# Attention block: probabilities turned by products with a diagonal of reciprocals instead of the identity

## The chip, the cores and the metric

One core of a Trainium2 chip runs the whole kernel. The metric is the device time of one execution in microseconds (us); the profile shows one execution, taken by the hardware profiler.

## The reference, cut to what matters

For x of shape (4, 1024, 1024) in f32, the block is `x + s * g`, where s is attention over the normalized x and g the SiLU of a feed-forward branch of the same input. The change concerns the attention alone:

```python
xn = _layernorm(x, axis=-1)
q = (xn @ Wq.T) ...        # 16 heads of 64, in 4 groups of 4 that share a key head
k, v = (xn @ Wk.T) ..., (xn @ Wv.T) ...
att = einsum('bkgqd,bkjd->bkgqj', q, k) * scale
mask = causal & (j >= i - 511) | (j < 4) ...   # window of 512 keys and 4 sink keys
att = softmax(where(mask, att, -inf), axis=-1)
y = einsum('bkgqj,bkjd->bkgqd', att, v)
s = y.reshape(b, t, c) @ Wo.T
```

The softmax divides each row of probabilities by its sum. That division can be made on the exponentials, or later on y, since every key of a query has the same divisor.

## The kernel before, in words

The work runs in stages: normalizing x and making keys and values (to about 270 us), queries and the gate (to 949 us), attention, with the small feed-forward branch for the last token streamed between its products (949 to 1741 us), and the output projection with the gated sum (to the end).

In the attention stage the queries are tiles of 128. Each batch has eight; they are taken in pairs (`PAIRED`), a *far* tile (tiles 7 to 4, whose window of 512 keys lies apart from the 4 sink keys) and a *near* tile (tiles 0 to 3, with 1 to 4 blocks of 128 keys). A *step* (class `Step`) treats, for such a pair of tiles, two query heads `r` of two key heads `g`; there are 16 pairs of tiles and 4 steps of each, 64 steps. The loop over `p` (L1317 on) writes out the order of all engines but SP by hand (`tc.manual_schedule`): while the values of step p are multiplied, the scores, maxima and exponentials of step p + 1 are made (`far_next`, `near_next`).

For a step the engines do this:

- `scored` (L277, products at L299): PE multiplies the queries (64 rows of a head as weights, 128 columns) by the keys, into the PSUM tile `S`. Where the near tile of the next step has at most two blocks of keys, its scores *ride* in the free columns of the far tile's `S` (`riding`, `ride`); this is so in 31 steps of the loop, and they have another order of work.
- `merged` and `maxed` (L314, L335): DVE merges the own block of a far tile and takes masked row maxima; it writes the negated scores to `pr` in SBUF.
- `powered` (L346): ACT makes the exponentials in place, and the row sums into `sums`.
- `sinks_kept` (L351): POOL copies the 4 sink columns of the exponentials into a zeroed tile `held`.
- `turned` (L369): PE turns blocks of 128 queries by 128 keys so that the keys lie on the partitions. `in_halves` does it in two halves of 64 queries, each a `transpose` of 64 rows of `pr` with the identity, into the PSUM tile `t`; ACT then copies `t` to `pT` in SBUF (L383). One call turns one or two blocks of keys, 8 transposes for each block.
- `values`, `values_apart` (L411, L427): PE multiplies `pT`, the sinks and a correction of the first block (`lead`) by the values, into the PSUM tile `yp`.
- `stored` (L434): DVE writes `yp` to SBUF, multiplied by the turned reciprocals `scales`; `sent` sends it to DRAM.

The reciprocals of the row sums come from `inverted` (L471): DVE inverts the 8 columns of sums of a step (far and near together), and POOL spreads each over 64 columns (tile `r`). `turned_extras` (L482) turns `held` and the four spread pieces, 10 transposes in a step, and ACT copies them to `extras` (tile `e`, 128x640, L497): its first part are the turned sinks, the others the `scales` that `stored` multiplies by. The turned pieces go to a PSUM tile of their own (`et`) in riding steps, and to the free columns of the next far tile's `S` in the others.

The feed-forward branch is a generator; `streamed(least, most)` puts some of its blocks of products on PE (L1099) at fixed places of a step, and `small_products` its small transposing products (L1161).

Of the kernel before, what the change touches and what calls it, by code (L numbers as in the profile page):

```python
# [8 lines left out]
F32 = mybir.dt.float32  # L9
AF = mybir.ActivationFunctionType  # L10
ALU = mybir.AluOpType
# [4 lines left out]
P = 128  # L16
N_HEAD = 16
N_KV = 4
HS = 64
# [25 lines left out]
def recurrent_block_kernel(  # L45
# [170 lines left out]
    def make_masks():  # L216
        first = pools["first"]

        m = masks["near"] = first.tile([P, SCOLS], F32, name="near_mask")
        nc.gpsimd.memset(m, 0.0)  # L220
        nc.gpsimd.affine_select(
            out=m[:, OWN:], in_=m[:, OWN:], compare_op=ALU.is_ge, fill=NEG,
            base=0, pattern=[[-1, P]], channel_multiplier=1,
        )
        masks["far"] = m[:, :OWN]
        masks["own"] = triangle(first, "own_keys", ALU.is_ge, 1)
        masks["lead"] = triangle(first, "lead_keys", ALU.is_gt, 1)

        m = masks["full"] = first.tile([P, SINK], F32, name="full_mask")
        nc.gpsimd.memset(m, 0.0)  # L230
        nc.gpsimd.affine_select(
            out=m, in_=m, compare_op=ALU.is_ge, fill=NEG,
            base=0, pattern=[[-1, SINK]], channel_multiplier=1,
        )
# [17 lines left out]
    class Step:  # L252
# [89 lines left out]
        def powered(self, *heads):  # L342

            for r, g in heads:
# [3 lines left out]
                    accum_out=self.sums[:, r, g : g + 1],  # L348
                )

        def sinks_kept(self):  # L351

            self.held = held_sinks[(PAIR * self.m + self.rp) % 2]
            nc.gpsimd.tensor_copy(
                self.held.rearrange("p (g r k) -> p g r k", g=2, r=PAIR)[
                    :, :, :, QUAD - SINK :
                ],
                self.pr[:, :, :, WINDOW:],
            )

        def in_halves(self, ps, slot, src, n):

            for h in range(2):
                rows = slice(h * HS, (h + 1) * HS)
                nc.tensor.transpose(  # L365
                    ps[:n, h, slot * HS : (slot + 1) * HS], src[rows], ident[rows, rows]
                )

        def turned(self, *keys):  # L369

            ps = pools["ps_t"].tile([P, 2, WIDE], F32, tag="T", name=f"t{self.name}_{keys[0]}")
            slots = 2 * PAIR * len(keys)
            for n, k in enumerate(keys):
                for g in range(2):
                    for r in range(PAIR):
                        self.in_halves(
                            ps, (n * 2 + g) * PAIR + r,
                            self.pr[:, g, r, k * P : (k + 1) * P], P,
                        )
            pT = pools["px"].tile(  # L380
                [P, 2, 2, PAIR * P], F32, tag="pT", name=f"pT{self.name}_{keys[0]}", bufs=2
            )
            nc.scalar.copy(  # L383
                pT.rearrange("p k g c -> p (k g c)")[:, : slots * P].rearrange(
                    "p (s h q) -> p h s q", h=2, q=HS
                ),
                ps[:, :, : slots * HS].rearrange("p h (s q) -> p h s q", q=HS),
            )
            for n, k in enumerate(keys):
                self.pT[k] = pT[:, n]  # L390
# [32 lines left out]
        def values_apart(self):  # L423

            for r in range(PAIR):
                for _, rows, cols in self.quads():
                    nc.tensor.matmul(  # L427
                        self.y[rows, r * P : (r + 1) * P],
                        sink_values[self.b][:, r, cols], self.extras[:, 0, :],
                        start=False, stop=False, skip_group_check=True,  # L430
                    )
            self.added(self.lead, leads[self.i], False, True)

        def stored(self):  # L434
            if self.rp == 0:
                state[self.i] = pools["px"].tile(
                    [P, GROUP, P], F32, tag="y", name=f"y{self.i}_{self.m}", bufs=3
                )
            at = self.rp * PAIR
            nc.vector.tensor_tensor(  # L440
                state[self.i][:, at : at + PAIR, :],
                self.y.rearrange("p (r q) -> p r q", r=PAIR), self.scales, ALU.mult,
            )

        def sent(self):
# [22 lines left out]
        y = pools["ps_y"].tile([P, 2, PAIR * P], F32, tag="y", name=f"yp{far.name}")  # L468
        far.y, near.y = y[:, 0, :], y[:, 1, :]

    def inverted(steps, sums):  # L471

        name = steps[0].name
        inverse = pools["px"].tile([P, 2 * PAIR * 2], F32, tag="inverse", name=f"i{name}", bufs=2)
        nc.vector.reciprocal(inverse, sums.rearrange("p s r g -> p (s r g)"))  # L475
        spread = pools["px"].tile([P, 2 * PAIR * 2, HS], F32, tag="spread", name=f"r{name}", bufs=1)
        nc.gpsimd.tensor_copy(  # L477
            spread, inverse.unsqueeze(2).to_broadcast([P, 2 * PAIR * 2, HS])
        )
        return spread.rearrange("p (s g) c -> p s (g c)", g=2)  # L480

    def turned_extras(steps, spread, behind):  # L482

        far, near = steps
        parts = [far.held, *(spread[:, s, :] for s in range(2 * PAIR))]
        if behind is None:
            ps = pools["ps_t"].tile([P, 2, WIDE], F32, tag="T", name=f"et{far.name}")
        else:
            ps = behind.S[:, 0, :, SCOLS:]
        for slot, src in enumerate(parts):  # L490
            far.in_halves(ps, slot, src, P)
        extras = pools["px"].tile([P, len(parts), P], F32, tag="extras", name=f"e{far.name}", bufs=1)
        far.extras = extras
        far.scales, near.scales = extras[:, 1 : 1 + PAIR, :], extras[:, 1 + PAIR :, :]

        def kept():
            nc.scalar.copy(  # L497
                extras.rearrange("p s (h q) -> p h s q", h=2),
                ps[:, :, : len(parts) * HS].rearrange("p h (s q) -> p h s q", q=HS),
            )  # L500

        return kept

    PLACE = {0: 0, 1: 1, 2: 2, 3: 4, 4: 5, 5: 6, 6: 3}
# [10 lines left out]
    with ExitStack() as a:  # L520
# [445 lines left out]
        with tc.manual_schedule():  # L966
# [4 lines left out]
            for at, (kind, pair) in enumerate(passes):  # L971
# [35 lines left out]
                for k, i in enumerate(OUTER):  # L1007
# [16 lines left out]
                    if end and k == 3:  # L1024
                        early.close()
                        second_banks.close()
                        pools["first"] = attention_only.enter_context(
                            tc.tile_pool(name="first", bufs=1, side="right")
                        )
                        pools["ps_s"] = attention_only.enter_context(  # L1030
                            tc.tile_pool(name="ps_s", bufs=1, space=PSUM, side="right")
                        )
                        attention_inputs()
                        (far, near), sums_now = steps_of(*order[0])
                        def scores(step, rs):
                            step.scored(rs)
                            step.merged(rs)
                            step.maxed(rs)
                            step.powered(*((r, g) for r in rs for g in range(2)))

                        first_scores = iter((
                            lambda: scores(far, (0,)), lambda: scores(far, (1,)),
                            far.sinks_kept, lambda: scores(near, both),
                        ))
            for part in first_scores:
                part()
# [11 lines left out]
    with ExitStack() as a:  # L1058
# [255 lines left out]
        with tc.manual_schedule(  # L1314
            engines={engines.PE, engines.DVE, engines.Activation, engines.Pool}
        ):
            for p in range(len(order)):  # L1317
# [56 lines left out]
                small_products(far_next.S if more else None)  # L1374
                if last_near is not None:
                    last_near.sent()
                if rode:
                    spread = inverted((far, near), sums_now)
                if more:
                    far_next.merged((0,))  # L1380
                    far_next.maxed((0,))
# [2 lines left out]
                if more:  # L1384
                    far_next.powered((0, 0))
                if not rode:
                    spread = inverted((far, near), sums_now)
                far.led()
                streamed(1, 1)
                summed_in_one_bank(far, near)  # L1390
# [2 lines left out]
                if ride:  # L1393
# [4 lines left out]
                    near_next.powered((0, 0), (0, 1))  # L1398
                    far_next.scored((1,))
                    near_next.riding(1, far_next)  # L1400
                    turned_extras((far, near), spread, None)()
                    far_next.merged((1,))
                    far_next.maxed((1,))
                    near_next.maxed((1,))
                    far_next.powered((1, 0), (1, 1))
                    near_next.powered((1, 0), (1, 1))
                    far_next.sinks_kept()
                    if n_near <= 2:
                        streamed(0, 2)
# [10 lines left out]
                else:  # L1420
                    far.turned(2, 3)
                    late_passes()
                    if more:
                        far_next.powered((0, 1))
                        far_next.scored((1,))
                    kept = turned_extras((far, near), spread, far_next if more else None)
                    if more:
                        far_next.merged((1,))
                    kept()
                    if more:  # L1430
                        far_next.maxed((1,))
                        far_next.powered((1, 0), (1, 1))
                        far_next.sinks_kept()
                    streamed(0, 1)
                    for k in (2, 3):
                        far.values(k)
                    far.values_apart()
                    far.stored()
                    far.sent()
                    near.turned(*range(min(2, n_near)))  # L1440
                    if more:
# [292 lines left out]
```

## Time and profile before

| | |
|---|---|
| time, median of 3 runs | 2139.3 us (2134.91 to 2139.39) |
| the profiled execution: its own time | 2139.05 us |
| the profiled execution: its span | 2137.3 us |
| TensorE (PE) busy | 2076.3 us |
| weight loads (PEld) busy | 1418.0 us |
| VectorE (DVE) busy | 1495.8 us |
| ScalarE (ACT) busy | 916.5 us |
| GpSimd (POOL) busy | 448.4 us |
| HBM | 202 GB/s over the span |

A row of a group in the profile reads: line, engine, operation, out<-in by the program's names, the tile of the array for products (rows * columns), the shape, xcount | busy us, mean ns of one | idle time of the engine just before, and what ended it. Busy time counts overlapping instructions once; the mean is the length of a single one, of which a product's pipeline is a part. `PEld` are the loads of weights into the array, which overlap the products (`PE`). In `t<-ident,pr` the second name, `pr`, is the operand that is loaded as weights, and `ident` the one that is streamed. A timeline row gives start, length, engine, line, operation and count of instructions that follow each other.

### The profile page before, as it was taken

What the parts mean: (1) busy time and instruction counts of PE and PEld (TensorE: products, weight loads), DVE (VectorE), ACT (ScalarE), POOL (GpSimd) and SP (SyncE); (2) the same over time, 40 slices, a digit from 0 to 9 for tenths busy, and PEclk for the clock granted to TensorE, in tenths of its full rate; (3) what the DMA queues carried; (4) which work ended last, traced back from release to release, by engine and by line L of the source; (5) the groups of instructions that cost most, each with busy time, mean ns of one, the idle gap of its engine ahead of it and who ended that gap; (6) DMA issues with size and microseconds to landing.
All of it is one profiled execution on the core that took longest, in us unless ns stands there. A gap on an engine that the chain in (4) does not pass through costs nothing.

```text
span 2137.3 us, 43582 instructions
## 1 busy us (share of the span) xinstructions
PE 2076.3 (97%) x17586; PEld 1418.0 (66%) x17586; DVE 1495.8 (70%) x3092; ACT 916.5 (43%) x1840; POOL 448.4 (21%) x641
## 2 busy tenths in 40 slices
PE   7999999999999999999999999999999989999999
PEld 6888888888888888875555655555565544444443
DVE  5867588888877888876556555666665547777766
ACT  4343212111110000037777777777777744333332
POOL 3232315435241021141111111111111101111111
PEclk9999999999999999999999999999999999999999
DMA  8696322433554234258778988768578536666653
GB/s 297 248 370 218 104 99 99 163 114 124 224 188 138 99 110 166 79 190 290 261 237 240 319 250 243 256 198 301 185 251 284 182 146 180 167 169 191 172 157 98
DMA packets 215201, 417.20 MB, mean 195 GB/s; under 512 B 13796, under 2 KB 97844, under 8 KB 209880
## 3 DMA queue, kind: packets, MB, share of 16 engines
q1 hardware_dynamic: 171432, 266.12, 38.8%
q0 software_dynamic: 28288, 91.41, 13.8%
q10 hardware_dynamic: 15280, 56.89, 7.1%
q8 instruction: 138, 2.26, 0.4%
q14 instruction: 63, 0.52, 0.1%
HBM read 309.22 MB, written 121.93 MB: 202 GB/s over the span
## 4 chain that ended last, share of the span: by engine, by line
PE 83%; DVE 6%; issue 4%; ACT 4%; POOL 2%; DMA 1%; SPq 0%; ACTq 0%; POOLq 0%; DVEq 0%
PE u L1572 17%; PE u_q L899 16%; PE u_g L899 13%; PE S L299 10%; PE yp L411 8%; PE d_ps L1099 6%; PE t L365 5%; PE u L679 4%; PE yp L427 1%; DVE pr L335 1%; ACT pr L346 1%; ACT pT L383 1%; DVE t_g L915 1%; DVE f L852 1%; PE xtp L595 1%
## 5 line engine op out<-in xcount | busy, mean ns | idle before, releaser
L346 ACT ACTIVATE pr<-pr,nm 128x516 f32<-128x516 f32 (+4 forms) x512 | 325.5, 638 | 86.8 <-DVE nm L335 85.7
L335 DVE CUSTOM_DVE_ANT_0 pr<-S,near_mask 128x516 f32<-128x516 f32 (+4 forms) x512 | 275.7, 590 | 98.2 <-PE S L299 56.0
L383 ACT COPY pT<-t 128x1024 f32<-128x1024 f32 (+1 forms) x224 | 212.0, 946 | 116.5 <-PE t L365 114.5
L299 PE MATMUL S<-kT,qT 64*128 64x512 f32 (+4 forms) x1536 | 246.4, 446 | 4.0 <-DVE i L475 2.4
L411 PE MATMUL yp<-pT,v 128*32 128x256 f32 x3328 | 215.2, 382 | 5.1 <-ACT pT L383 4.5
L899 PE MATMUL u_q<-f,wq_again 128*128 128x256 f32 x896 | 203.2, 379 | 0.0
L899 PE MATMUL u_g<-wg,f 128*128 128x256 f32 x864 | 195.7, 380 | 4.5 <-DVE t_g L915 4.5
L365 PEld LDWEIGHTS t<-ident,pr 64*128 64x128 f32 x3328 | 126.1, 140 | 90.6 <-issue 68.6
L411 PEld LDWEIGHTS yp<-pT,v 128*32 128x32 f32 x3328 | 104.1, 110 | 123.4 <-issue 51.7
L899 PEld LDWEIGHTS u_q<-f,wq_again 128*128 128x128 f32 x896 | 170.0, 190 | 23.3
L899 PEld LDWEIGHTS u_g<-wg,f 128*128 128x128 f32 x864 | 163.8, 190 | 28.2 <-DVE t_g L915 6.2
L299 PEld LDWEIGHTS S<-kT,qT 64*128 64x128 f32 x1536 | 127.6, 190 | 79.2 <-issue 69.8
L1572 PE MATMUL u<-wo_sb,y 128*128 128x512 f32 x384 | 170.1, 592 | 0.5 <-DVE y L440 0.5
L365 PE MATMUL t<-ident,pr 64*128 64x64 f32 x3328 | 153.1, 230 | 4.0 <-ACT pr L346 1.8
L314 DVE COPY_PREDICATED S<-own_keys,S 128x256 f32<-128x256 uint32 x128 | 54.9, 429 | 131.2 <-PE S L299 92.3
L945 ACT COPY t_q<-u_q 128x512 f32<-128x512 f32 x28 | 16.4, 586 | 275.4 <-PE u_q L899 275.4
L1572 PEld LDWEIGHTS u<-wo_sb,y 128*128 128x128 f32 x384 | 72.9, 190 | 92.4 <-issue 91.4
L915 DVE TENSOR_TENSOR t_q<-u_q,t_q 128x512 f32<-128x512 f32 x128 | 88.2, 689 | 63.8 <-PE u_q L899 49.3
L915 DVE TENSOR_TENSOR t_g<-u_g,t_g 128x512 f32<-128x512 f32 x128 | 87.9, 687 | 40.8 <-PE u_g L899 35.8
L1572 PE MATMUL u<-wo_t,s 128*128 128x512 f32 x256 | 112.5, 592 | 0.0
L346 ACT ACTIVATION_READ_ACCUMULATOR pr<-pr,nm 128x1 f32 x512 | 96.6, 189 | 0.0
L477 POOL COPY r<-i 128x512 f32<-128x512 f32 x64 | 47.7, 745 | 217.4 <-DVE i L475 208.0
(284 smaller groups left out, 3560.6 us busy)
## 6 DMA issues: line engine op xcount, KB each, us to landing
d_w<-in_d_w_dram SPq DMA_DIRECT2D x128, 1024.0 KB, 8.0
xT<-xT_dram SPq DMA_DIRECT2D x24, 1024.0 KB, 5.6
xn<-in_x_dram ACTq DMA_DIRECT2D x34, 512.0 KB, 5.4
xT_dram<-xT POOLq DMA_DIRECT2D x32, 512.0 KB, 6.0
qT<-q_dram SPq DMA_DIRECT2D x64, 256.0 KB, 5.8
y_dram<-y POOLq DMA_DIRECT2D x64, 256.0 KB, 5.8
y<-y_dram SPq DMA_DIRECT2D x32, 512.0 KB, 5.3
g<-g_dram SPq DMA_DIRECT2D x32, 512.0 KB, 11.2
```

The source lines that it names most:

```text
L299: nc.tensor.matmul(S[:, g, :], qTs[self.i, self.m][half, self.rp * PAIR + r, :], kT[half, self.m, keys, start:], start=True, stop=True,)
L314: nc.vector.copy_predicated(S[:, dst, :, 0:P], masks["own"].bitcast(mybir.dt.uint32).unsqueeze(1).to_broadcast([P, 2, P]), S[:, dst, :, OW ...
L335: nc.vector.tensor_tensor_reduce(out=low, in0=S[:, src, g, :cols], in1=self.mask, scale=-1.0 / HS**0.5, scalar=-NEG, op0=ALU.add, op1=ALU.min,
L346: nc.scalar.activation(low, low, AF.Exp, bias=self.maxima.pop((r, g)), scale=-1.0, accum_out=self.sums[:, r, g : g + 1],)
L365: nc.tensor.transpose(ps[:n, h, slot * HS : (slot + 1) * HS], src[rows], ident[rows, rows])
L383: nc.scalar.copy(pT.rearrange("p k g c -> p (k g c)")[:, : slots * P].rearrange("p (s h q) -> p h s q", h=2, q=HS), ps[:, :, : slots * HS] ...
L411: nc.tensor.matmul(self.y[rows, :], v[:, cols], pT[:, g, :], start=first, stop=last, skip_group_check=True,)
L679: nc.tensor.matmul(bank, left[n][i].rearrange("p a (k q) -> p a k q", k=2)[:, c // 2, c % 2, j * P : (j + 1) * P], kv7[i][:, c, :], start= ...
L899: nc.tensor.matmul(bank[:, t * QD : (t + 1) * QD], stationary[:, at : at + P], moving[:, c * QD : (c + 1) * QD], start=(first and c == 0 a ...
L915: nc.vector.tensor_add(dst, in0, in1)
L1099: nc.tensor.matmul(ps[j * QUAD : (j + 1) * QUAD, :], lhs[:, k, :], moving(w), start=(u == 0), stop=(u == len(blocks) - 1),)
L1572: nc.tensor.matmul(bank, left[n][i][:, c, j * P : (j + 1) * P], wo7[i][:, c, :], start=(first and c == 0), stop=(c == KH - 1), skip_group_ ...
```

## The change

The reciprocals enter where the exponentials are turned. The turning product streams, in place of 64 columns of the identity, a 64x64 diagonal whose entries are the reciprocals of the row sums (tile `diagonal`, for each head). It is an ordinary product now (`matmul`) and no longer a `transpose`. What leaves it is turned and normalized, so `stored` copies `yp` without a factor, and the spread reciprocals, their transposes and the `scales` are gone. The far sinks are multiplied by the reciprocals in `sinks_kept` (on POOL) before they are turned, still with a `transpose`, as the only part of the former extras.

A diagonal is made by `inverted`, now a method of `Step`: a reciprocal on DVE, and a product of a mask `eye` (two identities of 64, one under the other) with the reciprocals, on DVE for far tiles and on POOL for near ones. Far diagonals are made at the end of the step before (in riding steps in two parts, r = 0 and r = 1, before `far.stored`; in the others together, after it), near ones within the step, where the reciprocals were inverted before. `turned` now takes all blocks of r = 0 ahead of r = 1. In riding steps the sinks are turned into the free columns of the next far tile's `S`, too, and their copy comes after the merge.

```diff
+        eye = masks["eye"] = first.tile([P, HS], F32, name="eye")
+        nc.gpsimd.tensor_add(eye, ident[:, :HS], ident[:, HS:])
...
+        def inverted(self, rs, engine):
+            if rs[0] == 0:
+                tag, first = "far" if self.far else "near", pools["first"]
...
+            at, shape = slice(rs[0], rs[-1] + 1), [P, len(rs), 2, HS]
+            nc.vector.reciprocal(self.inverse[:, at, :], self.sums[:, at, :])
+            engine.tensor_tensor(
+                self.diagonal[:, at], masks["eye"].unsqueeze(1).unsqueeze(1).to_broadcast(shape),
+                self.inverse[:, at, :].unsqueeze(3).to_broadcast(shape), ALU.mult,
+            )
...
-            nc.gpsimd.tensor_copy(
+            nc.gpsimd.tensor_tensor(
                 self.held.rearrange("p (g r k) -> p g r k", g=2, r=PAIR)[
                     :, :, :, QUAD - SINK :
                 ],
                 self.pr[:, :, :, WINDOW:],
+                self.inverse.rearrange("p r g -> p g r").unsqueeze(3).to_broadcast(
+                    [P, 2, PAIR, SINK]
+                ),
+                ALU.mult,
+            )
...
+                dst = ps[:, h, slot * HS : (slot + 1) * HS]
+                if head is None:
+                    nc.tensor.transpose(dst, src[rows], ident[rows, rows])
+                else:
+                    nc.tensor.matmul(
+                        dst, src[rows], self.diagonal[rows, *head, :], start=True, stop=True
+                    )
...
-            for n, k in enumerate(keys):
-                for g in range(2):
-                    for r in range(PAIR):
+            for r in range(PAIR):
+                for n, k in enumerate(keys):
+                    for g in range(2):
...
-            nc.vector.tensor_tensor(
+            nc.vector.tensor_copy(
                 state[self.i][:, at : at + PAIR, :],
-                self.y.rearrange("p (r q) -> p r q", r=PAIR), self.scales, ALU.mult,
+                self.y.rearrange("p (r q) -> p r q", r=PAIR),
             )
...
-        parts = [far.held, *(spread[:, s, :] for s in range(2 * PAIR))]
...
-        for slot, src in enumerate(parts):
-            far.in_halves(ps, slot, src, P)
...
+            ps = behind.S[:, 0, :, at:]
+        far.in_halves(ps, 0, far.held)
...
+                            lambda: far.inverted(both, nc.vector), far.sinks_kept,
+                            lambda: scores(near, both),
+                            lambda: near.inverted(both, nc.gpsimd),
...
-                if rode:
-                    spread = inverted((far, near), sums_now)
+                if rode and p:
+                    near.inverted(both, nc.gpsimd)
...
-                    turned_extras((far, near), spread, None)()
+                    kept = turned_sinks(far, far_next, SCOLS + near_next.cols)
                     far_next.merged((1,))
+                    kept()
...
                     near_next.powered((1, 0), (1, 1))
+                    far_next.inverted((0,), nc.vector)
+                    far_next.inverted((1,), nc.vector)
                     far_next.sinks_kept()
...
                     far.values_apart()
                     far.stored()
+                    if more:
+                        far_next.inverted(both, nc.vector)
+                        far_next.sinks_kept()
                     far.sent()
```

More of the change, by code (lines that the diff above doesn't have):

```diff
@@ L349, in powered @@
                 )
+        def inverted(self, rs, engine):
+            if rs[0] == 0:
+                tag, first = "far" if self.far else "near", pools["first"]
+                self.inverse = first.tile(
+                    [P, PAIR, 2], F32, tag=f"{tag}_inverse", name=f"i{self.name}", bufs=2
+                )
+                self.diagonal = first.tile(
+                    [P, PAIR, 2, HS], F32, tag=f"{tag}_diagonal", name=f"d{self.name}", bufs=1
+                )
[5 more added lines that the diff above has]
+            )
         def sinks_kept(self):
             self.held = held_sinks[(PAIR * self.m + self.rp) % 2]
-            nc.gpsimd.tensor_copy(
+            nc.gpsimd.tensor_tensor(
                 self.held.rearrange("p (g r k) -> p g r k", g=2, r=PAIR)[
@@ L358, in sinks_kept, with in_halves @@
                 self.pr[:, :, :, WINDOW:],
+                self.inverse.rearrange("p r g -> p g r").unsqueeze(3).to_broadcast(
+                    [P, 2, PAIR, SINK]
+                ),
+                ALU.mult,
             )
-        def in_halves(self, ps, slot, src, n):
+        def in_halves(self, ps, slot, src, head=None):
             for h in range(2):
                 rows = slice(h * HS, (h + 1) * HS)
-                nc.tensor.transpose(
-                    ps[:n, h, slot * HS : (slot + 1) * HS], src[rows], ident[rows, rows]
-                )
+                dst = ps[:, h, slot * HS : (slot + 1) * HS]
[4 more added lines that the diff above has]
+                        dst, src[rows], self.diagonal[rows, *head, :], start=True, stop=True
+                    )
         def turned(self, *keys):
@@ L372, in turned @@
             slots = 2 * PAIR * len(keys)
-            for n, k in enumerate(keys):
-                for g in range(2):
-                    for r in range(PAIR):
+            for r in range(PAIR):
+                for n, k in enumerate(keys):
+                    for g in range(2):
                         self.in_halves(
                             ps, (n * 2 + g) * PAIR + r,
-                            self.pr[:, g, r, k * P : (k + 1) * P], P,
+                            self.pr[:, g, r, k * P : (k + 1) * P], (r, g),
                         )
@@ L428, in values_apart @@
                         self.y[rows, r * P : (r + 1) * P],
-                        sink_values[self.b][:, r, cols], self.extras[:, 0, :],
+                        sink_values[self.b][:, r, cols], self.held,
                         start=False, stop=False, skip_group_check=True,
@@ L469, in summed_in_one_bank, with turned_sinks @@
         far.y, near.y = y[:, 0, :], y[:, 1, :]
[L471 to L484, printed above, removed]
-        parts = [far.held, *(spread[:, s, :] for s in range(2 * PAIR))]
+    def turned_sinks(far, behind, at):
         if behind is None:
@@ L488, in turned_extras @@
         else:
-            ps = behind.S[:, 0, :, SCOLS:]
-        for slot, src in enumerate(parts):
-            far.in_halves(ps, slot, src, P)
-        extras = pools["px"].tile([P, len(parts), P], F32, tag="extras", name=f"e{far.name}", bufs=1)
-        far.extras = extras
-        far.scales, near.scales = extras[:, 1 : 1 + PAIR, :], extras[:, 1 + PAIR :, :]
+            ps = behind.S[:, 0, :, at:]
+        far.in_halves(ps, 0, far.held)
+        sinks = pools["px"].tile([P, P], F32, tag="held", name=f"e{far.name}", bufs=1)
+        far.held = sinks
         def kept():
[L497 to L500, printed above, removed]
+            nc.scalar.copy(sinks.rearrange("p (h q) -> p h q", h=2), ps[:, :, :HS])
         return kept
@@ L1042, in recurrent_block_kernel @@
                             lambda: scores(far, (0,)), lambda: scores(far, (1,)),
-                            far.sinks_kept, lambda: scores(near, both),
+                            lambda: far.inverted(both, nc.vector), far.sinks_kept,
+                            lambda: scores(near, both),
+                            lambda: near.inverted(both, nc.gpsimd),
                         ))
@@ L1386, in recurrent_block_kernel @@
                 if not rode:
-                    spread = inverted((far, near), sums_now)
+                    near.inverted(both, nc.gpsimd)
                 far.led()
@@ L1425, in recurrent_block_kernel @@
                         far_next.scored((1,))
-                    kept = turned_extras((far, near), spread, far_next if more else None)
+                    kept = turned_sinks(far, far_next if more else None, SCOLS)
                     if more:
@@ L1432, in recurrent_block_kernel @@
                         far_next.powered((1, 0), (1, 1))
-                        far_next.sinks_kept()
                     streamed(0, 1)
```

## The prediction

> **What bounds the kernel now.** I read the page first (shares, then the chain that ended last), then the busy times by stretch, then the groups by shape for each operation that the change touches, and last the timeline around two of the steps.
>
> ```profile
> span 2137.3 us, 43582 instructions
> ...
> PE 2076.3 (97%) x17586; PEld 1418.0 (66%) x17586; DVE 1495.8 (70%) x3092; ACT 916.5 (43%) x1840; POOL 448.4 (21%) x641
> ...
> PE 83%; DVE 6%; issue 4%; ACT 4%; POOL 2%; DMA 1%; SPq 0%; ACTq 0%; POOLq 0%; DVEq 0%
> ```
>
> TensorE is busy 97% of the span and is 83% of the chain. The tiles that change (`t`, `e`, `held`, `yp`) occur from 949 to 1741 us, the attention stage. Its row among the stretches (engines in the order PE, PEld, DVE, ACT, POOL, then clock, DMA share, GB/s):
>
> ```profile
> 949.00:1741.00 792.00, 763.34 (x12290) 443.50 (x12290) 468.04 (x1546) 589.31 (x1308) 112.22 (x221) 0.99 0.75 242
> ```
>
> PE leaves 792.0 - 763.3 = 28.7 us of 792 uncovered; DVE is busy 59%, ACT 74%, POOL 14%. Microseconds added to PE in this stage are microseconds of the kernel; work added to DVE or POOL costs only where PE waits for its result. Hence two questions: what one turning product costs on PE, and who waits for the diagonal.
>
> ```profile
> L365 PE MATMUL t<-ident,pr 64*128 64x64 f32 x3328 | 153.1, 230 | 4.0 <-ACT pr L346 1.8 <-ACT pT L383 1.1 <-DVE t_q L915 0.8
> L365 PEld LDWEIGHTS t<-ident,pr 64*128 64x128 f32 x3328 | 126.1, 140 | 90.6 <-issue 68.6 <-ACT pT L383 13.6 <-ACT pr L346 2.8
> L299 PEld LDWEIGHTS S<-kT,qT 64*128 64x128 f32 x1536 | 127.6, 190 | 79.2 <-issue 69.8 <-PE t L365 4.1 <-DVE nm L335 1.2
> L299 PE MATMUL S<-kT,qT 64*128 64x128 f32 x128 | 12.3, 272 | 0.0
> L365 PE MATMUL S<-ident,r 64*128 64x64 f32 x256 | 13.7, 223 | 0.0
> L365 PE MATMUL et<-ident,r 64*128 64x64 f32 x256 | 13.5, 223 | 0.0
> L497 ACT COPY e<-S 128x640 f32<-128x640 f32 x32 | 22.1, 690 | 10.6 <-DVE S L321 8.1 <-DVE S L314 1.6
> L475 DVE RECIPROCAL i<-s 128x8 f32<-128x8 f32 x64 | 12.6, 197 | 4.6 <-ACT pr L346 4.5
> ```
>
> A transpose holds the probabilities as weights and streams 64 columns of the identity. Its weight load takes 140 ns; an ordinary f32 load of the same 64x128 shape (the scores, L299) takes 190.
>
> **The change part by part.** *The turning products.* The two halves of a head, rows 0-63 and 64-127, run side by side, so I count pairs: 3328 instructions are 1664 pairs. Pacing comes from the timeline:
>
> ```profile
> 1203.28 0.57 PEld L365 LDWEIGHTS t<-ident,pr 64*128 64x128 f32 x16 [0.41 <-issue]
> 1203.28 0.71 PE L365 MATMUL t<-ident,pr 64*128 64x64 f32 x16
> 1203.83 1.74 PE L299 MATMUL S<-kT,qT 64*128 64x512 f32 x12
> ```
>
> Eight pairs take 0.55 us until the scores begin, 69 ns each with the slower first one; from start to start of the single records the median is 63 ns. The weight row of 16 loads is as long as the block (0.57 us): loading 128 columns, not streaming 64, sets this pace. After the change each is an ordinary f32 product: load 64x128, stream 64. The nearest row is the score product of the shortest near tiles, an ordinary load of 64x128 with 128 columns streamed. Its busy time is 12.3/128 = 96 ns, so four in a row (two pairs) cover 384 ns; less the 272 of the last, 112 ns lie between pairs (109 as the median of the single starts). The load fits within that 109. Streaming 64 columns instead of 128 cannot make it dearer, and makes it cheaper only if the load is well below 109. It is not likely to be: the load grew by 190 - 140 = 50 ns over the transposing one, and 63 + 50 = 113. I take 109, with 113 as the upper bound. Cost: 1664 x (109 - 63) = **+76.5 us**, all on PE in a stage where PE covers 96%.
>
> The Trainium skill speaks against this edit: "Perfetto Trace Analysis", section Transposes, asks that logical transposes use the transpose and not a standard matmul, and "TensorE: Matmul & The Clock Gate", section Terms, calls the transposing mode four times faster for FP32. By the four, an estimate from that page, a pair would go from 63 to 252 ns and the sum would be 1664 x 189 = 314 us, near 2440 us in all; the trace's rows differ by less than two, and I go by the rows.
>
> *The turned reciprocals.* 512 transposes (`r`) go, 256 pairs x 63 = **-16.1 us** of PE. The sinks' two transposes per step stay, and with them the gap before the next kind of product.
>
> *The copy of the extras.* ACT copies 128x128 instead of 128x640: 690 ns becomes about 300 (an exponential on 128x128 takes 392, a 128x512 copy 586), 64 x 0.39 = 25 us less ACT. PE waits for this copy directly only 10.1 us in 9 places, where ACT is late for other reasons and PE now comes 0.25 us sooner: **-2 us**.
>
> *The diagonals.* Near: a reciprocal on DVE where one was (197 ns), and on POOL a 128x256 product in place of a 128x512 copy (745 ns; POOL's 128x512 two-input product takes 1638, half of it 0.82). Its reader, `near.turned`, comes over 3 us later, after scores, a streamed block and `far.values`: nothing. Far: DVE gains one or two reciprocals and 128x256 of product (two-input DVE rows: 0.42 us for 256, about 0.29 for 128), some 50 us in all against 324 us of idle. In the steps without riding this follows `far.stored`, where DVE then stands idle 1.2 to 1.75 us for the near scores; the exponentials end 2.4 us or more before `far.turned`: nothing.
>
> In the 31 riding steps there is little room. In a step whose near tile has one block:
>
> ```profile
> 1164.75 0.40 PE L365 MATMUL t<-ident,pr 64*128 64x64 f32 x6
> 1165.34 0.39 ACT L346 ACTIVATE pr<-pr,nm 128x128 f32<-128x128 f32 x1
> 1165.48 0.39 PEld L365 LDWEIGHTS t<-ident,pr 64*128 64x128 f32 x10 [0.47 <-ACT pr L346]
> ```
>
> Six transposes start at 1164.75, the others wait until the last far exponential is out, 1165.43. That step is already paced by scores, maxima and exponentials (DVE and ACT), not by PE. The diagonal now adds to this chain: 0.05 to pass on, 0.19 reciprocal, 0.03, 0.28 product, 0.05: 0.6 us. The new order (r = 0 first, four pairs) covers some where PE is the later. By the starts of `far.turned` against the ends of the exponentials, 10 of the 16 one-block steps and 2 of the 12 two-block steps have negative slack, 3 have 0.2 us, the rest 0.6 or more. With 0.25 us less of extras on PE the three lose 0.45: 12 x 0.6 + 3 x 0.45 = 8.6, **+9 us**. Behind the waiting reciprocals DVE also holds back the small sums of the FFN (means, variances) in some ten places, about 1 us late against a streamed block 2 us on: **+2 us**.
>
> *The output.* A copy from PSUM for a product from PSUM (421 ns) is the same pass on DVE: 0. The first step's diagonals fall in the stage before and are five small instructions: 0.
>
> Sum: 76.5 - 16.1 - 2 + 9 + 2 = +69.4 us. The profiled execution's own time is 2139.05 (its span 2137.3 and 1.75 around it), which stands 0.25 below the median of 2139.3. **2139.05 + 69.4 = 2208 us.**
>
> **The rivals.** *Faster: a diagonal product is paced like a transpose.* If an ordinary load is hidden when only 64 columns follow, pairs stay at 63, the first term is nil and -16.1 - 2 + 11 = -7 is left: 2132 us. It decides below 63 + 7.1/1.664 = 67 ns a pair. For it: the profile has no ordinary 64x128 load with fewer than 128 columns behind it. Against: 16 loads already fill the block, and the ordinary one is 50 ns longer. 3%.
>
> *Load and product do not overlap.* A pair costs 109 plus half of it for streaming, 163: +166, 2298 us. Against: in the score rows load and 128 columns together fit in 109. 3%.
>
> *The chain through DVE binds in every riding step*: DVE takes maxima, two reciprocals, two products and the stores in order, the sinks' copy on ACT now precedes the maxima, and all 31 lose 0.9 us instead of 12 losing 0.6: +19, 2227 us. For it: 0.6 us of slack in most. Against: PE becomes later by 0.4 us in each block of 16. 17%.
>
> *PE's added time covers old waits*: half of the 28.7 us of uncovered PE time vanishes and the diagonals cost nothing, 2208 - 14 - 9 = 2185 us. Against: in the one-block steps the waiting engine is not PE's rival but its supplier, and that supply gets longer. 12%.
>
> **How the numbers follow.** My forecast has 65%. The low end is the last rival, 2185; the high end takes the third rival and 113 ns a pair (+6.7), 2234. Left out are the two extreme pairings and the tails, under 2 in 10. A measurement of this kernel tells about 0.2% (4 us) from no change. Faster only by the first rival: 0.03; within 4 us 0.01; slower 0.96.
>
> **What would show it.** Right: the group of `t` has mean weight loads of 190 ns, eight pairs take about 0.9 us, and the attention stage is 65 to 75 us longer with the others unchanged; PE rows of `t` wait for DVE in riding steps, about 0.5 us each. Wrong: pair starts near 63 (first rival) or beyond 150 (second), or a stage longer by less than 55 us with the pairs at 109, which would mean that old waits were covered.

## The result, and the profile after

The changed kernel takes 2406.7 us (median of 4 runs, 2391.55 to 2407.63) against 2139.35: 1.1236 times the time, 95% interval 1.1189 to 1.1284. I had forecast 2208, at most 2234. The direction was right and the size was far off: +267 us where I had +69.

The page of the changed kernel, the same lines as before:

```profile
span 2404.8 us, 49510 instructions
...
PE 2341.2 (97%) x20402; PEld 1679.0 (70%) x20402; DVE 1537.4 (64%) x3282; ACT 895.8 (37%) x1840; POOL 458.9 (19%) x642
...
PE 86%; DVE 6%; issue 4%; ACT 2%; POOL 2%; DMA 0%; SPq 0%; POOLq 0%; ACTq 0%; DVEq 0%
```

TensorE still sets the time. The count says what happened: 17586 products became 20402, although the change removes 512 transposes and adds no product in the source. The stages before and after attention are nearly as they were: attention starts at 949 us in both, and what follows it takes 394 us before and 391 now. Attention itself takes 270.6 us longer. Its rows among the stretches (PE, PEld, DVE, ACT, POOL, clock, DMA share, GB/s), before and after, each to the end of its last product, and the groups of the turning products:

```profile
949.00:1743.40 794.40, 765.03 (x12307) 444.22 (x12308) 468.80 (x1548) 589.72 (x1308) 112.39 (x223) 0.99 0.75 242
949.00:2014.00 1065.00, 1029.60 (x15123) 705.18 (x15124) 512.18 (x1737) 569.02 (x1308) 123.36 (x223) 0.97 0.55 181
```

```profile
L393 PE MATMUL t<-d,pr 64*128 64x64 f32 x6656 | 427.1, 278 | 19.2 <-DVE i L365 8.3 <-DVE d L366 7.8 <-ACT pT L411 1.2
L393 PEld LDWEIGHTS t<-d,pr 64*128 64x128 f32 x6656 | 404.0, 192 | 104.2 <-issue 76.7 <-PE yp L439 14.7 <-ACT pT L411 9.4
```

3328 products are 6656 records: an ordinary f32 product is *two* loads of weights and two streams, where the transpose was one of each. Busy time of the group goes from 153.1 to 427.1 us. The timeline shows the pace, eight pairs of halves in one block:

```profile
1300.14 2.00 PE L393 MATMUL t<-d,pr 64*128 64x64 f32 x32
1301.97 0.65 PE L302 MATMUL S<-kT,qT 64*128 64x512 f32 x2
```

```profile
1300.13 1.86 PEld L393 LDWEIGHTS t<-d,pr 64*128 64x128 f32 x32 [0.41 <-issue]
```

The block takes 1.83 us until the scores begin; it took 0.55. The loads fill it again from end to end (1.86 us). From start to start of the single records the median is 112 ns between one record and the next on the same half, so a pair costs 224 ns, not 109.

### The profile page after: what moved, and what is told of

The parts are those of the page before. It is cut to its first block, busy times and chain, and to the rows that moved or that the text cites. A ratio compares the mean times of both kernels' runs of the same rounds, so it can differ in the third digit from the quotient of the medians.

```text
span 2404.8 us, 49510 instructions
## 1 busy us (share of the span) xinstructions
PE 2341.2 (97%) x20402; PEld 1679.0 (70%) x20402; DVE 1537.4 (64%) x3282; ACT 895.8 (37%) x1840; POOL 458.9 (19%) x642
## 4 chain that ended last, share of the span: by engine, by line
PE 86%; DVE 6%; issue 4%; ACT 2%; POOL 2%; DMA 0%; SPq 0%; POOLq 0%; ACTq 0%; DVEq 0%
PE t L393 17%; PE u L1585 16%; PE u_q L905 14%; PE u_g L905 12%; PE S L302 9%; PE yp L439 8%; PE d_ps L1107 5%; PE u L685 3%; DVE pr L338 2%; PE yp L455 1%; ACT pT L411 1%; DVE t_g L921 1%; DVE f L858 1%; PE xtp L601 1%; POOL moments L115 1%
## 5 line engine op out<-in xcount | busy, mean ns | idle before, releaser
L393 PEld LDWEIGHTS t<-d,pr 64*128 64x128 f32 x6656 | 404.0, 192 | 104.2 <-issue 76.7
L393 PE MATMUL t<-d,pr 64*128 64x64 f32 x6656 | 427.1, 278 | 19.2 <-DVE i L365 8.3
L921 DVE TENSOR_TENSOR t_q<-u_q,t_q 128x512 f32<-128x512 f32 x128 | 88.2, 689 | 63.1 <-PE u_q L905 48.6
L374 POOL TENSOR_TENSOR held<-pr,i 128x16 f32<-128x16 f32 x64 | 22.8, 356 | 502.5 <-DVE i L365 502.5
L366 POOL TENSOR_TENSOR d<-eye,i 128x256 f32<-128x256 f32 x64 | 47.6, 744 | 311.5 <-DVE i L365 309.6
```

The costliest lines, as they stand in the source:

```text
L393: nc.tensor.matmul(dst, src[rows], self.diagonal[rows, *head, :], start=True, stop=True)
L921: nc.vector.tensor_add(dst, in0, in1)
```

## The experiments

**Only the product.** The kernel before, with one edit:

```diff
...
-                nc.tensor.transpose(
-                    ps[:n, h, slot * HS : (slot + 1) * HS], src[rows], ident[rows, rows]
-                )
+                nc.tensor.matmul(dst, src[rows], ident[rows, rows], start=True, stop=True)
...
```

(for the probabilities; the spread reciprocals and the sinks stay transposes.)

> The kernel before, with one edit: the 3328 turning transposes of the probabilities are ordinary products with the same identity; the reciprocals are turned and applied as before. Theory (an ordinary f32 product is two load-and-product records, 112 ns for each pair of halves, so a pair goes from 63 to 224 ns): 1664 x 161 = +268 us, near 2405 us, weight loads and products of the tile t counted 6656 each. Rival (the product costs the 109 ns that I forecast, and the rest of the 267 us is waiting for the diagonals): 1664 x 46 = +77 us, near 2216 us.

Measured: 2397.7 us, 1.1217 times before (1.118 to 1.1254). No diagonal exists in this kernel, and it is still 258 us slower. Its groups:

```profile
L367 PE MATMUL t<-ident,pr 64*128 64x64 f32 x6656 | 424.1, 277 | 1.9 <-ACT pT L385 1.2 <-DVE t_q L917 0.8
L367 PEld LDWEIGHTS t<-ident,pr 64*128 64x128 f32 x6656 | 400.3, 191 | 85.7 <-issue 73.5 <-ACT pT L385 9.4 <-DVE t_q L917 1.2
```

The count doubles with the kind of instruction alone, and PE waits for next to nothing. The loss is in the product.

**Everything but the product.** The changed kernel, with `head` left out in `turned`, so that it transposes with the identity:

```diff
-                            self.pr[:, g, r, k * P : (k + 1) * P], (r, g),
+                            self.pr[:, g, r, k * P : (k + 1) * P],
```

> The kernel after, but turned by transposes with the identity; the diagonals are still made but nobody waits for them, and the division is left out of the result. It holds everything of the change but the product. Theory: the 512 transposes of the spread reciprocals are gone (-16 us) and the smaller copy gives about 2: 2119 to 2125 us. Rival (the new order of the queues, with reciprocals, diagonals and the sinks' copy ahead of the maxima, costs by itself): 2130 us or more.

Measured: 2127.4 us, 0.9953 times before (0.9934 to 0.9972): 12 us gained, between the two expectations. The spread reciprocals are worth their 16 us (from start to start 22.7 us of transposes go, and the sinks' take 6.5 more), but some of it comes back: the blocks of `t` take 6.8 us more in sum (144.3 us from the first start to the next kind of product, against 137.5), and PE waits for exponentials longer than the 1.8 us of before:

```profile
L391 PE MATMUL t<-ident,pr 64*128 64x64 f32 x3328 | 155.2, 230 | 8.2 <-ACT pr L349 5.3 <-ACT pT L411 1.2 <-DVE t_q L921 0.8
```

This is the most that a free division could be worth in this order of the queues.

**The product without the wait.** The changed kernel, streaming the constant `eye`:

```diff
-                        dst, src[rows], self.diagonal[rows, *head, :], start=True, stop=True
+                        dst, src[rows], masks["eye"][rows], start=True, stop=True
```

> The kernel after, but the turning products stream the constant two identities instead of the diagonal; diagonals are still made, nobody waits for them, and the division is left out of the result. Theory: the products cost the same, and only the waits of PE for the diagonals go, 17 us by the profile (8.3 and 7.8 for DVE, 1.1 for POOL): 2388 to 2400 us. Rival (waiting for the diagonals makes up most of what I did not forecast): near 2216 us.

Measured: 2381.4 us, 1.1135 times before (1.11 to 1.1171), a little below the lower end. The steps from kernel to kernel are then: -12.0 for all but the product, +253.9 for the product, +25.3 for the diagonals that PE waits for, together +267.2. The last number holds more than waiting. This kernel's and the changed kernel's runs each fall into two groups by the granted clock: 2374.6 and 2376.1 us at 0.993 and 2386.6 and 2387.2 at 0.988 here, 2391.6 at 0.993 and 2406.6 to 2407.6 at 0.986 to 0.987 there. At the same clock (0.993, where the changed kernel has a single run) the diagonals cost 16 us, and the rest goes with the clock. The +253.9 holds some clock too: the trace's clock record has the kernel with transposes at half of the full clock for 20 us and this one for 34.5 us, which is worth up to 7 us. The rows of the changed kernel for the wait itself:

```profile
PE t L393 <- DVE i L365: 8.3, 10, 1.5
PE t L393 <- DVE d L366: 7.8, 8, 1.2
```

**Half the records, twice the columns.** One product of 128 rows and a diagonal of 128 columns for each block, in place of two halves:

```diff
...
-                        self.in_halves(
-                            ps, (n * 2 + g) * PAIR + r,
-                            self.pr[:, g, r, k * P : (k + 1) * P], (r, g),
-                        )
+                        bank, at = divmod((n * 2 + g) * PAIR + r, WIDE // P)
+                        nc.tensor.matmul(
+                            ps[:, bank, at * P : (at + 1) * P],
+                            self.pr[:, g, r, k * P : (k + 1) * P], self.diagonal[:, r, g, :],
+                            start=True, stop=True,
+                        )
...
```

> The kernel after, with one product of 128x128 weights and a 128x128 diagonal for a block, in place of two halves of 64 rows with 64 columns each: half as many records, twice the columns streamed by each, and a diagonal twice as wide (some 0.3 us more on DVE for a step). Theory (the load of 128 columns sets the pace, 112 ns for each of the two records): a block stays at 224 ns, 2400 to 2415 us. Rival A (each record costs 56 ns to issue): 1664 x 112 = 186 us less, near 2220 us. Rival B (the columns streamed set the pace): a block doubles, near 2780 us.

Measured: 2431.1 us, 1.1368 times before (1.1346 to 1.139). The group has half the records and nearly the same busy time:

```profile
L405 PE MATMUL t<-d,pr 128*128 128x128 f32 x3328 | 434.6, 283 | 22.1 <-DVE i L365 9.5 <-DVE d L366 8.9 <-POOL d L366 1.5
```

A block costs 223 ns from start to start (two records of 111.5), with half the records and twice the columns of each. Both rivals fall as they were put: the time follows neither the number of records nor the columns of each. It is slower than expected. Part of that is the blocks' ends: summed over 223 runs of turning products, the first gap is 22.4 us over the pace instead of 6.8, and the way from the last product to the next kind 50.2 us instead of 36.9, together 29 us that the halves had hidden. The 24 us between the two kernels understate the loss, since this one ran at a clock of 0.997 and the changed kernel mostly at 0.986 to 0.987 (17 us at half clock in the profiled run against 69). What is left beyond the ends at one clock, up to some 20 us, is not traced to a cause.

**Twice the loads, the same columns.** Each product split into the first and the last 32 columns of the diagonal:

```diff
+                    for c in (slice(0, HS // 2), slice(HS // 2, HS)):
                         nc.tensor.matmul(
-                        dst, src[rows], self.diagonal[rows, *head, :], start=True, stop=True
+                            dst[:, c], src[rows], self.diagonal[rows, *head, c],
+                            start=True, stop=True,
...
```

> The kernel after, with each turning product split in two, of the first and the last 32 columns of the diagonal: twice the records, the same columns streamed in all, the same result. Theory (the load of 128 columns of weights paces each record, however few columns follow): a pair of halves goes from 4 to 8 records, 224 to 448 ns, 1664 x 224 = +373 us, near 2780 us. Rival (the columns streamed set the pace): 2407 us.

Measured: 3069.1 us, 1.4358 times before (1.4329 to 1.4387). The records double and the median from start to start stays at 112 ns at full clock, with 32 columns as with 64 and 128. A fixed price of each record could give this row, too, but not the others: f32 transposes pass two records in 63 ns, and products with the same f32 records but loads of only 32 columns take less still. Of these, 32 records, 16 products in the source, pass in 0.28 us in the kernel before (four stand side by side in the array, so a group of four takes 35 ns):

```profile
1200.28 0.44 PE L1161 MATMUL S<-sel,d_sb 128*32 128x8 f32 x32
1200.56 1.06 PE L1099 MATMUL d_ps<-d_w,t_cols 128*32 128x512 f32 x8
```

What the products at 112 ns have in common is that each record loads 128 columns of f32 weights for an ordinary product: that is the pace.

The time is nearly 290 us beyond the expectation, and for that the row of the stretch shows the reason, a granted clock of 0.80 in the whole attention stage:

```profile
L394 PE MATMUL t<-d,pr 64*128 64x32 f32 x13312 | 896.4, 292 | 15.9 <-DVE d L366 7.3 <-DVE i L365 6.7 <-ACT pT L413 1.1
949.00:2674.00 1725.00, 1696.90 (x21788) 1259.41 (x21786) 515.13 (x1739) 570.78 (x1308) 124.28 (x223) 0.80 0.36 113
```

The trace's clock record knows full speed and half of it, nothing between. This run stands at half for 686 us, and there the median step is 213 ns. Every product of the stage pays for it: from start to start, the turning products take 463 us more than in the changed kernel, where 373 were reckoned, and the others some 200 us more.

**In bf16.** Exponentials written as bf16 (in the place of the f32 scores) and bf16 diagonals:

```diff
...
+            self.prb = self.pr.bitcast(mybir.dt.bfloat16)
...
-                    low, low, AF.Exp, bias=...
+                    self.prb[:, g, r, : self.cols], low, AF.Exp, bias=...
...
```

> The kernel after, with the exponentials and the diagonals rounded to bf16, so that the turning product is an ordinary product of bf16 operands; all else in f32. Theory (the price is that an f32 product takes two records and two passes in each): 3328 records for the tile t, a pair at 63 ns or less, and what is left is the 25 us that the wait for the diagonals costs on top of 2127: 2120 to 2155 us. Rival (any ordinary product is dear beside a transpose, whatever its type): 2350 us or more.

Measured: 2103.7 us, 0.9835 times before (0.9817 to 0.9852).

```profile
L394 PE MATMUL t<-d,pr 64*128 64x64 bf16 x3328 | 92.7, 191 | 24.6 <-DVE d L367 18.8 <-POOL d L367 2.0 <-ACT pT L412 1.7
```

One record for each product again, 29 ns for a pair, and the ordinary product is cheaper than the transpose in f32. What is dear is f32 in an ordinary product, not the ordinary product itself. PE now arrives early and waits for the diagonals (18.8 us).

**The price of that wait in bf16**, with a constant bf16 `eye` streamed:

> The version with bf16 exponentials and diagonals, but streaming a constant bf16 identity: the diagonals are made and nobody waits for them, the division is left out of the result. Theory (the wait for the diagonals costs the 16 us that it costs in f32 at the same clock, or more, since PE arrives earlier): 2104 less 16 to 32, 2072 to 2088 us. Rival (the wait is mostly covered): 2095 to 2104 us.

Measured: 2095.5 us, 0.9801 times before (0.9785 to 0.9817). That is 8 us less, at the edge of the rival's range and outside the theory's: the wait is mostly covered. The 20.8 us of idle time before the diagonals in the row above are not all recovered.

**The bf16 product without any diagonal**: the kernel before, bf16 exponentials, a bf16 identity, reciprocals turned and applied as before.

> The kernel before, with the exponentials rounded to bf16 and turned by ordinary bf16 products with a bf16 identity; the reciprocals are made, turned and applied as before, in f32. Theory (a bf16 turning product costs 30 ns for a pair instead of 63, and without diagonals PE has less to wait for): 1664 x 33 = 55 us less, of which the riding steps, paced by their exponentials, give some back: 2085 to 2098 us, faster than the version with bf16 diagonals (2104). Rival (the chain of maxima and exponentials now binds in most steps, whoever divides): 2104 us or more.

Measured: 2106.5 us, 0.9852 times before (0.9836 to 0.9868). The time lies where the rival put it: the products were reckoned 55 us cheaper and only 31 arrive, and the two ways of dividing can't be told apart (2103.7 and 2106.5). The rival's reason is seen in part only. PE waits longer for reciprocals, maxima and exponentials, but only by some 6 us in all (the rows of this kernel stood at 2.4, 1.3 and 1.8 us before):

```profile
PE S L303 <- DVE i L481: 5.6, 11, 0.9
PE S L303 <- DVE nm L339: 3.4, 9, 0.7
PE t L373 <- ACT pr L350: 2.8, 7, 0.5
```

In the profiled run, which is this kernel's fastest (2100.4 us), the blocks of `t` take 48.6 us less from the first start to the next kind of product, not 55. What else takes the difference is not traced.

**The order of the turning.** The changed kernel with keys, then g, then r, as before:

> The kernel after, with the turning products in the order of before (keys, then g, then r), so that the second product already needs the diagonal of r = 1. Theory (the order r = 0 first covers up to four pairs, now 0.9 us, of the wait for the last diagonal in the riding steps): 0.2 to 0.5 us in each of 31 steps, 2413 to 2423 us. Rival (the wait is for something else, or PE is late anyway): 2391 to 2408 us, as after.

Measured: 2412.9 us, 1.129 times before (1.125 to 1.133), at the edge of what was expected, and its runs spread with the clock: 2404.4 and 2405.3 at 0.991, 2420.4 and 2421.5 at 0.984. Between the changed kernel's two points (2391.6 at 0.993, 2406.7 at 0.9865) a straight line gives 2396 at 0.991, so r = 0 first is worth about 9 us. That is worked out over the clock, not measured at one.

**Two other ways to divide**, from the kernel before: the near tiles' probabilities scaled in SBUF ahead of their transposes, half of the spread reciprocals gone.

```diff
...
+        for r in range(PAIR):
+            for g in range(2):
+                part, at = near.pr[:, g, r, : near.cols], 2 * PAIR + 2 * r + g
+                nc.gpsimd.tensor_scalar(part, part, inverse[:, at : at + 1], None, ALU.mult)
...
```

> The kernel before, with the near tiles' probabilities multiplied by their reciprocals in SBUF, on POOL in four pieces, ahead of their transposes; the far tiles keep the turned reciprocals. Transposes stay transposes; 4 instead of 8 spread pieces are turned in a step. Theory (a division that costs PE nothing is worth what it removes from PE): 128 pairs x 63 = 8 us, and 2 to 4 us from the smaller copy: 2127 to 2132 us. Rival (POOL's four pieces, some 0.75 us each for 512 columns by its copy, come late for the near transposes or slow DVE): 2140 us or more.

Measured: 2369.6 us, 1.1085 times before (1.1068 to 1.1101). POOL needs twice what I took from its copy, and the far tiles' spread reciprocals queue behind the pieces:

```profile
L484 POOL TENSOR_SCALAR pr<-pr,i 128x512 f32<-128x512 f32 x64 | 102.9, 1620 | 105.8 <-DVE i L478 105.8
```

```profile
PE S L365 <- POOL r L485: 136.4, 31, 5.6
```

The clock adds to it: with these waits the run stands at half for 211 us (0.956 over the execution).

The same on DVE:

> As the version with the near tiles scaled on POOL, but on DVE: four pieces of up to 512 columns, 0.3 to 0.7 us each, in its queue right after the reciprocals and ahead of the lead's product. Theory: the same 8 us of PE, if DVE, busy 59% of the attention stage, has the room: 2127 to 2135 us. Rival (DVE sits in the chain of maxima and exponentials, and what is put before them is paid in the riding steps): 2140 to 2170 us.

Measured: 2156.5 us, 1.0092 times before (1.0077 to 1.0107). Its pieces are short (321 to 513 ns), but they stand ahead of the work that feeds the exponentials: PE's wait for the maxima grows from 1.3 to 13.6 us. The rival holds, and dividing the near tiles in SBUF at this place in the queue is no way to the 12 us.

## Why the prediction was wrong

The failing step is the first term, the price of a turning product. I wrote that the score products' "busy time is 12.3/128 = 96 ns, so four in a row (two pairs) cover 384 ns; less the 272 of the last, 112 ns lie between pairs". The 112 was right, and it is the pace of the changed kernel to the nanosecond. But I took the 128 records for 128 products. The shortest near tiles occur in 16 steps with 4 score products each: 64 products, and the row says x128. The four in a row were one pair of products, each in two records. The same check was open on every f32 row that I showed: the scores are 12 products in a step (8 far, 4 near), 768 in 64 steps, and the row says x1536; the transposes are 3328 in the source and 3328 in the row. The timeline line of the prediction shows "x12" for six score products.

By its own steps:

- *Turning products*: 1664 x (109 - 63) = +76.5 should have been 1664 x (224 - 63) = +268. Measured +253.9 between the kernels with transposes and with a constant diagonal, of which 252.4 lie in the blocks of `t` themselves (144.3 to 396.7 us from the first start to the next kind of product).
- *The page that spoke against it*: 63 to 252 ns for a pair by the factor four of "TensorE: Matmul & The Clock Gate", section Terms. Measured 224, a factor of 3.6, and the 2440 us that this estimate led to lay nearer to the 2406.7 than my forecast. I had set the rule aside because the rows "differ by less than two"; they did, for one record of two.
- *The signs*: of those named for "right", weight loads of 190 ns came (192) beside eight pairs in 1.83 us and not 0.9. The length of a load does not tell how many loads a product has.
- *Load or stream*: that loading sets the pace was right, shown by 112 ns a record for 32, 64 and 128 columns. The rival in which load and product do not overlap was wrong for the same reason as the forecast: it too counted one record.
- *The turned reciprocals and the copy*: -16.1 and -2. The kernel with everything but the product gains 12. The copy takes 262 ns (I took 300), and PE waits 8.8 us for it instead of 10.1.
- *The diagonals*: sizes as forecast (0.42 and 0.29 us on DVE; 0.74 on POOL, where I had 0.82; their rows stand below), in riding steps as forecast, but +9 us was 16 at the same clock: PE waits 18 times, 0.9 us on average, where I had 15 waits of at most 0.6. The near diagonals cost 1.1 us of waiting, nearly the nothing that I gave them.

```profile
L366 DVE TENSOR_TENSOR d<-eye,i 128x128 f32<-128x128 f32 x62 | 18.1, 292 | 2.1
L366 DVE TENSOR_TENSOR d<-eye,i 128x256 f32<-128x256 f32 x33 | 14.0, 425 | 1.2
L366 POOL TENSOR_TENSOR d<-eye,i 128x256 f32<-128x256 f32 x64 | 47.6, 744 | 311.5 <-DVE i L365 309.6
```

- *The clock*: not in the sum at all; some 9 of the last 25 us, and a part of the +253.9.
- *The small sums of the FFN*, +2 us, were not tried apart.

## What to carry to other kernels

Before a price is read off a row, hold its count against the source: where the profile has twice the records, one operation costs twice the row. A transpose in f32 is one load and one stream, an ordinary f32 product two of each; with up to 128 columns streamed, the load of the weights set the whole price here. In bf16 the price fell to an eighth (29 ns for 224). Where PE sets the time, work that is to ride on an f32 transpose is not free if it turns the transpose into an ordinary f32 product.

The fastest kernel here that divides is the change with bf16 exponentials and diagonals, 2103.7 us, 1.7% below the kernel before; it rounds the probabilities to bf16. The kernel with a bf16 identity can't be told from it, so the gain is that of the bf16 product and not of the diagonals. In f32 no version that divides beat the kernel before.

## What the runs showed of the hardware

- The granted clock falls while PE is busy all the time. With weights loaded at the same pace, 128 columns on all rows kept 0.997 over the execution, two halves of 64 columns 0.984 to 0.995, two halves of 32 columns 0.888 (0.80 in the stage), with PE counted busy 97 to 98% of the span in the profiles:

```profile
core 0: 3065.9 us, clock 0.888
```

The clock is full or half, in stretches of 3.41 us and multiples of it; the profiled runs of the three stand at half for 17, 69 (the changed kernel) and 686 us. "TensorE: Matmul & The Clock Gate", Part 1, has a monitor that gates the clock by how busy PE has been, and gives pauses as the reason. Here the pauses are not what the profile calls idle: from 955 to 968 us of the run with 32 columns PE counts as busy for all 13 us, at a clock of 0.50.

An estimate from the traces fits columns streamed as what counts, and not loads. An f32 record of 512 columns starts 429 ns after the one before it (products of the output projection), 0.84 ns a column. At this price the array streams for 0.46 (median, at most 0.56) of the 3.41 us ahead of each of the 103 drops of the run with 32 columns, while PE counts as busy for 1.00 (median). The 566 stretches after which the clock stays full stream for more than 0.56 in all but 21 cases. This goes by what stands together in the traces; no run varies the streaming alone.

- POOL multiplies 128x512 by one scalar for each partition in 1620 ns, and copies as much in 745.
